# A state-space layer and a spectral layer on one core: stores moved to another queue, deeper loads, constants loaded ahead, and one image kept on the chip between the last stages

## The chip, the core and the metric

The kernel runs on one core of one Trainium2 chip. The time is device microseconds of the whole execution; the median of the runs counts. The profiled execution is a run of its own, with its own time.

The core's engines are TensorE (PE, matmuls; PEld is its weight load), VectorE (DVE), ScalarE (ACT), GpSimd (POOL) and SyncE (SP), which here only issues DMAs. Each engine works through its own queue in order. A DMA is issued by an instruction in one engine's queue and carried out by 16 DMA engines that all queues share.

## The reference, cut to what matters

Two layers on x of 4 images x 128 channels x 128 x 128 in float32. The first is a windowed state-space (Mamba) layer, which the change leaves alone. The second is this:

```python
z = (x - mu) / jnp.sqrt(var + 1e-05)          # over the channels
z = z * ln_gamma + ln_beta
Xf = jnp.fft.rfft2(z, axes=(-2, -1))          # 128 x 65 frequencies
Uf = Xf[:, :, None] * jnp.conj(Phi)[None, None]   # 16 filters Phi
U = jnp.fft.irfft2(Uf, s=(gx, gy), axes=(-2, -1))
S = jnp.einsum('bdlxy,lhd->bhxy', U, Theta)   # 16 matrices Theta, 128 x 128
H = jnp.einsum('bdxy,hd->bhxy', S, W1) + b1
H = jax.nn.gelu(H)
out = x + jnp.einsum('bhxy,dh->bdxy', H, W2) + b2
```

As everything up to S is linear, the kernel mixes the channels in the frequency domain: for each of the 65 frequency rows it multiplies the spectrum by the 16 Thetas and sums the products weighted by Phi, and transforms back only the sum.

## The kernel before, in words

Four functions run one after the other and hand over through DRAM.

`mamba_layer` (L34) writes the first layer's output `x1` and the normalised `z`, one DRAM tensor for each image (`zb[b]`). All of its loads and stores go through SP's queue.

`spectra` (L470) transforms one image after the other. For each image it goes through the 128 channels in groups of DG = 16; `load` (L493) brings one group's z tile (128 x 16 x 128, 1 MB, in rows of 512 bytes) two groups ahead, into three buffers. `along_x` (L499) takes four channels at a time: matmuls into a PSUM tile `p1`, then one copy into `a` (L504). `copies` alternates between ScalarE and VectorE. When all channels are in `a`, `along_y` (L506) transforms along y, three columns at a time, into a PSUM tile `p2`, and ScalarE copies its real half and VectorE its imaginary half into `x` (L517). `p1` and `p2` have four buffers each. `x` holds half an image's columns (q = 0 or 1); after each half it is stored to `xf` in one DMA of 4160 KB on SP's queue (L533), in rows of 512 bytes.

`mix` (L536) loads Theta and Phi (L549 to L552), then loops over the 65 rows. A row's `xk` is loaded two rows ahead in two DMAs (L561). For each of 16 filters PE multiplies (L584), and the results are weighted and summed by VectorE into `acc` (L599, L601), or, for six of the filters, weighted by ScalarE into `part` (L595) and summed by GpSimd into `apart` (L597). `finish` (L563) adds the two sums (L566) and stores the row for each image and half to `sf` in eight DMAs of 64 KB (L570). It runs after filter 5 of the next row, and once more after the last row.

`images_and_mlp` (L608) loads its constants (L624 to L630) and, for each image, the two halves of the mixed spectrum, 4160 KB each (L636), two buffers deep. `reorder` (L638) puts 16 channels at a time in order, ScalarE and VectorE sharing the work (L645 to L647); `along_x` (L649) and `along_y` (L661) transform back, and `hidden` and `project` are the MLP. The residual `x1` is loaded into `mx` (L665), the result is summed into `mo` (L688) and stored (L690).

Each function opens its own pools of on-chip memory and closes them at its end; the next function's pools take over the same memory. Waits are put in by the framework, from what each instruction reads and writes. `manual_schedule` keeps the order of the work near that in which the code lists it.

Of the kernel before, what the change touches and what calls it, by code (L numbers as in the profile page):

```python
# [13 lines left out]
F32 = mybir.dt.float32  # L14
# [7 lines left out]
WS = 8  # L22
# [5 lines left out]
HB = 512  # L28
NL = 16
KY = W // 2 + 1  # L30
NG = WS * W // P


def mamba_layer(tc, d, x, x1, zb, deltas, dus):  # L34
# [432 lines left out]
            go(lates.get(s, ()))  # L467


def spectra(tc, d, zb, xf):  # L470

    nc = tc.nc
    B = len(zb)
    DG = 16
    CG, KG = HB // W, HB // (2 * KY)
    WH = W // 2  # L480
    with ExitStack() as ctx:
        ctx.enter_context(tc.manual_schedule())
        cp = ctx.enter_context(tc.tile_pool(name="f_const", bufs=1))
        sb = ctx.enter_context(tc.tile_pool(name="f_sb", bufs=2))
        ps = ctx.enter_context(tc.tile_pool(name="f_ps", bufs=4, space=PSUM))
        fx = cp.tile([P, W], F32, tag="fx", name="fx")
        nc.sync.dma_start(fx, d["dft_x"])
        fy = cp.tile([P, 4 * KY], F32, tag="fy", name="fy")
        nc.sync.dma_start(fy, d["dft_y"])
        loaded = {}  # L490
        copies = itertools.cycle((nc.scalar.copy, nc.vector.tensor_copy))

        def load(b, i):  # L493
            b, i = b + i // P, i % P
            if b < B:
                loaded[b, i] = sb.tile([P, DG, W], F32, tag="z", name="z", bufs=3)
                nc.sync.dma_start(loaded[b, i], zb[b][i : i + DG].rearrange("c x y -> x c y"))

        def along_x(b, i, a):  # L499
            z = loaded[b, i - i % DG]  # L500
            p1 = ps.tile([P, CG, W], F32, tag="p1", name="p_fx")
            for k in range(CG):
                nc.tensor.matmul(p1[:, k], z[:, i % DG + k], fx, start=True, stop=True)
            next(copies)(a[:, :, i : i + CG].rearrange("p k c -> p c k"), p1)  # L504

        def along_y(a, x, cols):  # L506
            p2 = ps.tile([P, KG, 2 * KY], F32, tag="p2", name="p_fy")
            for o, k in zip(range(KG), cols):
                m = min(k, W - k)
                single = m % WH == 0  # L510
                nc.tensor.matmul(p2[:, o], a[:, m], fy[:, KY : 3 * KY], start=True, stop=single)
                if not single:
                    by = fy[:, : 2 * KY] if m == k else fy[:, 2 * KY :]
                    nc.tensor.matmul(p2[:, o], a[:, WH + m], by, start=False, stop=True)
            n, at = len(cols), cols[0] % WH
            for r in range(2):
                next(copies)(  # L517
                    x[:, :, r, at : at + n].rearrange("p y k -> p k y"), p2[:, :n, r * KY : (r + 1) * KY]
                )

        load(0, 0)
        load(0, DG)
        for b in range(B):
            a = sb.tile([P, W, P], F32, tag="a", name="a", bufs=1)
            for i in range(0, P, CG):
                if i % DG == 0:
                    load(b, i + 2 * DG)
                along_x(b, i, a)
            for q in range(2):
                x = sb.tile([P, KY, 2, WH], F32, tag="x", name="x")  # L530
                for k in range(q * WH, (q + 1) * WH, KG):
                    along_y(a, x, range(k, min(k + KG, (q + 1) * WH)))
                nc.sync.dma_start(xf[:, :, b, q].rearrange("y c r x -> c y r x"), x)  # L533


def mix(tc, d, xf, sf):  # L536

# [4 lines left out]
    APART = (1, 4, 6, 9, 12, 14)  # L542
    with ExitStack() as ctx:
        ctx.enter_context(tc.manual_schedule())
        cp = ctx.enter_context(tc.tile_pool(name="m_const", bufs=1))
        sb = ctx.enter_context(tc.tile_pool(name="m_sb", bufs=3))
        ps = ctx.enter_context(tc.tile_pool(name="m_ps", bufs=4, space=PSUM))
        theta = cp.tile([P, NL, P], F32, tag="theta", name="theta")
        nc.sync.dma_start(theta, d["Theta"])  # L549
        phi = cp.tile([P, 3, NL, KY], F32, tag="phi", name="phi")  # L550
        nc.sync.dma_start(phi[:, 0], d["Phi_r"])
        nc.sync.dma_start(phi[:, 1], d["Phi_i"])  # L552
        nc.vector.tensor_scalar(phi[:, 2], phi[:, 1], -1.0, None, ALU.mult)
        rows = {}

        def load(y):
            if y < KY:
                rows[y] = o = SimpleNamespace()
                o.xk = sb.tile([P, B, 2, 2, W // 2], F32, tag="xk", name="xk")
                for q in range(2):  # L560
                    nc.sync.dma_start(o.xk[:, :, :, q], xf[y, :, :, q])  # L561

        def finish(y):  # L563
            if y >= 0:
                o = rows.pop(y)
                nc.vector.tensor_tensor(o.acc, o.acc, o.apart, ALU.add)  # L566
                at = y - 1 if 0 < y < KY - 1 else KY - 2 + y // (KY - 1)
                for b in range(B):
                    for q in range(2):
                        nc.sync.dma_start(sf[b][:, q, at], o.acc[:, b, :, q * (P // 2) : (q + 1) * (P // 2)])  # L570

        load(0)
        load(1)
        for y in range(KY):
            o = rows[y]
# [29 lines left out]
        finish(KY - 1)  # L605


def images_and_mlp(tc, d, sf, x1, out):  # L608

# [7 lines left out]
    n = WS * W  # L617
    with ExitStack() as ctx:
        ctx.enter_context(tc.manual_schedule())
        cp = ctx.enter_context(tc.tile_pool(name="i_const", bufs=1))  # L620
        sb = ctx.enter_context(tc.tile_pool(name="i_sb", bufs=2))
        ps = ctx.enter_context(tc.tile_pool(name="i_ps", bufs=2, space=PSUM))
        ix = cp.tile([P, 2 * W], F32, tag="ix", name="ix")
        nc.sync.dma_start(ix, d["idft_x"])  # L624
        iy = cp.tile([P, W], F32, tag="iy", name="iy")
        nc.sync.dma_start(iy, d["idft_y"])
        c = {}
        for k in ("W1", "b1", "W2", "b2"):
            c[k] = cp.tile(list(d[k].shape), F32, tag=k, name=f"c_{k}")
            nc.sync.dma_start(c[k], d[k])  # L630
        spec, ordered, px, rows = {}, {}, {}, {}

        def load(b, q):
            if b < B:
                spec[b, q] = sb.tile([P, KY, 2, HP], F32, tag="s", name="s")
                nc.sync.dma_start(spec[b, q], sf[b][:, q])  # L636

        def reorder(b, i):  # L638
# [43 lines left out]
        def project(b, k, g):  # L682
            o = rows[b, k // 2]
            hs = slice(k % 2 * HB, (k % 2 + 1) * HB)
            po = ps.tile([P, HB], F32, tag="po", name="p_o")
            for m in range(2):
                nc.tensor.matmul(po, c["W2"][:, m], g[:, m], start=(m == 0), stop=(m == 1))  # L687
            nc.vector.scalar_tensor_tensor(o.o[:, hs], po, c["b2"], o.x[:, hs], ALU.add, ALU.add)  # L688
            if k % 2:
                nc.sync.dma_start(out[b][:, o.at].rearrange("c x y -> c (x y)"), o.o)  # L690
# [114 lines left out]
```

## Time and profile before

| | |
|---|---|
| median of 3 runs | 10520.61 us (10503.9 to 10534.1) |
| profiled execution, its own time | 10535.09 us |
| its span, first to last instruction | 10533.3 us |
| `mamba_layer`, about | 0 to 7273 us |
| `spectra`, PE's part | 7281 to 7683 us, PE busy 352.0 of 401 us |
| seam to `mix` | 7683 to 7709 us, PE busy 0.06 of 26 us |
| `mix`, PE's part | 7709 to 9711 us, PE busy 1941 of 2002 us |
| seam to `images_and_mlp` | 9711 to 9738 us, PE busy 0.8 of 27 us |
| `images_and_mlp` | 9738 to 10533 us, PE busy 786 of 796 us |

The profile is one execution. Its timeline lists instructions in order of time: start, duration, engine, line, what is written from what, how often, and in square brackets how long the engine had been idle and what released it. SPq and ACTq are the DMA issues in the queues of SP and ACT; the duration there is that of issuing, not of moving the data. The chain that ended last is followed back from the last instruction, at each step to what released it. A stretch lists for each engine its busy time and count, then the clock granted to TensorE as a share of full speed, the busy share of the DMA engines, and GB/s.

### The profile page before, as it was taken

To read this page: it belongs to the slowest core of one execution; us is meant where nothing else is said; L and a number is where in the kernel's file an instruction comes from. 1 tells how busy PE (TensorE), PEld (TensorE's weight loads), DVE (VectorE), ACT (ScalarE), POOL (GpSimd) and SP (SyncE) were. 2 spreads that over 40 slices of the span, in tenths; PEclk is the share of its full clock that TensorE was granted. 3 is DMA by queue.
4 is the path that set the end of the run, shared out by engine and by line. 5 is a ranking of instruction groups with operands and counts; after the bars stand their busy time and mean duration, and the time that the engine had idled before them with its cause. 6 is when DMAs were issued, how large, how long until landed. Compare 5 with 4: busy or idle time off the path is not lost.

```text
span 10533.3 us, 134916 instructions
## 1 busy us (share of the span) xinstructions
PE 9299.8 (88%) x46084; PEld 4658.4 (44%) x46084; DVE 9052.1 (86%) x7299; ACT 6333.5 (60%) x9711; POOL 8393.2 (80%) x4380
## 2 busy tenths in 40 slices
PE   7888888888888888888888888888889999998999
PEld 2222222222222222222222222224889999998766
DVE  6999999999999999999999999996379999998433
ACT  5766766766666666667667666664344444444433
POOL 5999899899999998999998999994069999998000
PEclk9999999999999999999999999998999999999999
DMA  5777777777777777777777777775621111112332
GB/s 156 210 216 210 207 215 211 207 218 206 214 216 205 216 211 204 221 212 208 215 211 207 216 207 216 214 205 159 169 69 35 35 35 35 35 35 63 133 128 93
DMA packets 1149630, 1759.95 MB, mean 167 GB/s; under 512 B 366592, under 2 KB 434448, under 8 KB 1147792
## 3 DMA queue, kind: packets, MB, share of 16 engines
q1 hardware_dynamic: 1148944, 1751.32, 58.7%
q8 instruction: 367, 6.01, 0.2%
q14 instruction: 319, 2.61, 0.1%
HBM read 1447.89 MB, written 303.04 MB: 166 GB/s over the span
## 4 chain that ended last, share of the span: by engine, by line
PE 46%; DVE 29%; ACT 12%; issue 6%; POOL 5%; DMA 2%; DVEq 0%; SPq 0%; ACTq 0%; POOLq 0%
DVE hs L416 19%; PE p_v L584 13%; PE p_conv L203 9%; DVE p_du L414 8%; ACT part L595 5%; PE p_du L382 4%; POOL hs L424 3%; PE p_out L275 2%; PE p_h L678 2%; PE p_o L687 2%; ACT dA L397 2%; PE p_y L434 2%; ACT p_du L397 2%; PE p_out L273 2%; PE p_in L189 1%
## 5 line engine op out<-in xcount | busy, mean ns | idle before, releaser
L424 POOL TENSOR_TENSOR hs<-hs,bc 128x1024 f32<-128x1024 f32 x2048 | 4797.4, 2361 | 469.8 <-DVE hs L416 464.9
L416 DVE TENSOR_TENSOR_SCAN hs<-dA,p_du 128x1024 f32<-128x1024 f32 x1664 | 3805.0, 2287 | 219.2 <-DVE p_du L414 3.4
L597 POOL TENSOR_TENSOR acc<-acc,part 128x512 f32<-128x512 f32 x1430 | 1829.3, 1319 | 615.3 <-ACT part L595 615.3
L414 DVE TENSOR_TENSOR p_du<-p_du,bc 128x1024 f32<-128x1024 f32 x1664 | 2014.8, 1211 | 273.9 <-PE p_du L382 270.1
L397 ACT ACTIVATE dA<-dr,A 128x504 f32<-128x504 f32 x3328 | 2156.0, 703 | 104.5 <-DVE hs L416 86.8
L584 PE MATMUL p_v<-theta,xk 128*128 128x128 f32 x16640 | 1941.4, 277 | 87.3 <-ACT part L595 51.4
L584 PEld LDWEIGHTS p_v<-theta,xk 128*128 128x128 f32 x16640 | 1883.1, 192 | 145.6 <-ACT part L595 118.3
L382 PE MATMUL p_du<-du,c_rsel 32*128 32x512 f32 x6656 | 1515.6, 662 | 478.6 <-DVE hs L416 473.4
L601 DVE SCALAR_TENSOR_TENSOR acc<-p_v,phi,acc 128x512 f32<-128x512 f32 x2470 | 1672.8, 741 | 114.3 <-PE p_v L584 87.4
L595 ACT ACTIVATE part<-p_v,phi 128x512 f32<-128x512 f32 x1430 | 903.7, 685 | 804.4 <-PE p_v L584 802.1
L434 PE MATMUL p_y<-hs,c_ssel 128*32 128x512 f32 x8192 | 1176.0, 642 | 189.3 <-DVE yz L264 185.7
L203 PE MATMUL p_conv<-tn,W_conv 128*128 128x512 f32 x2048 | 1007.5, 616 | 132.6 <-ACT zs L194 127.2
L382 PEld LDWEIGHTS p_du<-du,c_rsel 32*128 32x128 f32 x6656 | 409.1, 187 | 1532.1 <-issue 1004.7
L362 POOL TENSOR_TENSOR ur<-ur,bc 128x1024 f32<-128x1024 f32 x384 | 908.0, 2365 | 7.2 <-DMA ur<-du 7.2
L416 DVE TENSOR_TENSOR_SCAN hs<-p_du,ur 128x1024 f32<-128x1024 f32 x384 | 870.9, 2268 | 42.1 <-ACT p_du L397 29.4
L208 ACT ACTIVATE xc<-p_conv,b_conv 128x512 f32<-128x512 f32 x256 | 176.3, 689 | 829.2 <-PE p_conv L203 829.2
L434 PEld LDWEIGHTS p_y<-hs,c_ssel 128*32 128x32 f32 x8192 | 176.7, 110 | 1032.7 <-issue 728.6
L203 PEld LDWEIGHTS p_conv<-tn,W_conv 128*128 128x128 f32 x2048 | 347.0, 189 | 584.7 <-ACT zs L194 281.8
L228 PE MATMUL p_dt<-xc,W_dt 128*128 128x512 f32 x1024 | 535.0, 647 | 75.8 <-ACT dl L239 71.1
L218 PE MATMUL p_bc<-xc,c_W_bc 128*128 128x512 f32 x1024 | 501.3, 612 | 113.9 <-ACT dl L239 66.3
L397 ACT ACTIVATE p_du<-dr,A 128x504 f32<-128x504 f32 x768 | 526.1, 685 | 25.0
L246 POOL TENSOR_TENSOR dl<-dl,ab 128x1024 f32<-128x1024 f32 x128 | 303.3, 2370 | 178.1 <-ACT ab L243 178.1
(102 smaller groups left out, 9762.3 us busy)
## 6 DMA issues: line engine op xcount, KB each, us to landing
dr<-delta SPq DMA_DIRECT2D x4096, 256.0 KB, 4.8
ur<-du SPq DMA_DIRECT2D x768, 256.0 KB, 5.9
delta<-dl SPq DMA_DIRECT2D x128, 512.0 KB, 3.0
du<-du SPq DMA_DIRECT2D x128, 512.0 KB, 4.4
xf<-x SPq DMA_DIRECT2D x8, 4160.0 KB, 16.4
xk<-xf SPq DMA_DIRECT2D x130, 256.0 KB, 3.7
sf<-acc SPq DMA_DIRECT2D x520, 64.0 KB, 1.7
s<-sf SPq DMA_DIRECT2D x8, 4160.0 KB, 13.5
```

The costliest lines, as they stand in the source:

```text
L203: nc.tensor.matmul(windows(o.pc), W_conv[:, ch, k], moved, start=(k == 0), stop=(k == K - 1))
L362: nc.gpsimd.tensor_tensor(fetched[s], fetched[s], both(o.bc[0], h), ALU.mult)
L382: nc.tensor.matmul(u.bank[:, j % 2], c["rsel"][p, u.i], half(u.o.du[p, u.ch], u.h), start=True, stop=True)
L397: nc.scalar.activation(u.dA[:, q, :, 1:], u.delta[:, q].rearrange("p (w t) -> p w t", t=L)[:, :, 1:], AF.Exp, scale=A[:, g : g + 1],)
L414: nc.vector.tensor_tensor(u.bu, u.bu, both(u.o.bc[0], u.h), ALU.mult)
L416: nc.vector.tensor_tensor_scan(u.hs.rearrange("p q t -> p (q t)"), u.dA.rearrange("p q w t -> p (q w t)"), u.bu.rearrange("p q t -> p (q t)"),
L424: nc.gpsimd.tensor_tensor(u.hs, u.hs, both(u.o.bc[1], u.h), ALU.mult)
L434: nc.tensor.matmul(o.py[h, ch][32 * j : 32 * j + 32], c["ssel"][:, u.i], units[s + j // 2].hs[:, j % 2], start=(u.i == 0), stop=False, ski ...
L584: nc.tensor.matmul(t[:, b], o.xk[:, b, r], theta[:, k], start=True, stop=True)
L595: nc.scalar.activation(part, v[of], AF.Copy, scale=factor)
L597: nc.gpsimd.tensor_tensor(apart, apart, part, ALU.add)
L601: nc.vector.scalar_tensor_tensor(mine, v[of], factor, mine, ALU.mult, ALU.add)
```

## The change

In `spectra`, z is loaded four groups ahead instead of two, into five buffers instead of three. `xf` becomes five DRAM tensors of 13 rows each, and the half image's store becomes five DMAs issued by ScalarE. `mix` and `images_and_mlp` get their constants from tiles that are loaded during the first image's `spectra`, except Phi, which `mix` now loads after its first row. The first image's mixed rows go into two on-chip tiles `kept`, which `images_and_mlp` uses as its first two spectrum buffers; so `finish` adds in three pieces and stores three images instead of four. `images_and_mlp` sums into `mx`, which has three buffers instead of two, and `mo` is gone.

```diff
@@ spectra
-    DG = 16
+    DG, AHEAD = 16, 4
...
-                loaded[b, i] = sb.tile([P, DG, W], F32, tag="z", name="z", bufs=3)
+                loaded[b, i] = sb.tile([P, DG, W], F32, tag="z", name="z", bufs=AHEAD + 1)
...
-        load(0, 0)
-        load(0, DG)
+        for i in range(AHEAD):
+            load(0, i * DG)
...
-                    load(b, i + 2 * DG)
+                    load(b, i + AHEAD * DG)
                 along_x(b, i, a)
+            if b == 0:
+                preload()
             for q in range(2):
                 x = sb.tile([P, KY, 2, WH], F32, tag="x", name="x")
                 for k in range(q * WH, (q + 1) * WH, KG):
                     along_y(a, x, range(k, min(k + KG, (q + 1) * WH)))
-                nc.sync.dma_start(xf[:, :, b, q].rearrange("y c r x -> c y r x"), x)
+                for g, rows in enumerate(xf):
+                    nc.scalar.dma_start(rows[:, :, b, q].rearrange("y c r x -> c y r x"), x[:, g * YG : (g + 1) * YG])
@@ mix
-        theta = cp.tile([P, NL, P], F32, tag="theta", name="theta")
-        nc.sync.dma_start(theta, d["Theta"])
-        phi = cp.tile([P, 3, NL, KY], F32, tag="phi", name="phi")
...
+        theta = c["Theta"]
...
-                    nc.sync.dma_start(o.xk[:, :, :, q], xf[y, :, :, q])
+                    nc.sync.dma_start(o.xk[:, :, :, q], xf[y // YG][y % YG, :, :, q])
...
-                nc.vector.tensor_tensor(o.acc, o.acc, o.apart, ALU.add)
                 at = y - 1 if 0 < y < KY - 1 else KY - 2 + y // (KY - 1)
-                for b in range(B):
+                for q in range(2):
+                    hs = slice(q * (P // 2), (q + 1) * (P // 2))
+                    nc.vector.tensor_tensor(kept[q][:, at], o.acc[:, 0, :, hs], o.apart[:, 0, :, hs], ALU.add)
+                nc.vector.tensor_tensor(o.acc[:, 1:], o.acc[:, 1:], o.apart[:, 1:], ALU.add)
+                for b in range(1, B):
                     for q in range(2):
                         nc.sync.dma_start(sf[b][:, q, at], o.acc[:, b, :, q * (P // 2) : (q + 1) * (P // 2)])
         load(0)
+        phi = sb.tile([P, 3, NL, KY], F32, tag="phi", name="phi", bufs=1)
+        nc.sync.dma_start(phi[:, 0], d["Phi_r"])
+        nc.sync.dma_start(phi[:, 1], d["Phi_i"])
+        nc.vector.tensor_scalar(phi[:, 2], phi[:, 1], -1.0, None, ALU.mult)
         load(1)
@@ images_and_mlp
-        spec, ordered, px, rows = {}, {}, {}, {}
+        spec, ordered, px, rows = {(0, q): t for q, t in enumerate(kept)}, {}, {}, {}
...
-                spec[b, q] = sb.tile([P, KY, 2, HP], F32, tag="s", name="s")
+                spec[b, q] = sp.tile([P, KY, 2, HP], F32, tag="s", name="s")
...
-                o.x = sb.tile([P, n], F32, tag="mx", name="mx")
+                o.x = sb.tile([P, n], F32, tag="mx", name="mx", bufs=3)
...
-                o.o = sb.tile([P, n], F32, tag="mo", name="mo")
...
-            nc.vector.scalar_tensor_tensor(o.o[:, hs], po, c["b2"], o.x[:, hs], ALU.add, ALU.add)
+            nc.vector.scalar_tensor_tensor(o.x[:, hs], po, c["b2"], o.x[:, hs], ALU.add, ALU.add)
...
-        load(0, 0)
-        load(0, 1)
@@ conv_kernel
-    xf = tc.dram_tile([KY, P, B, 2, 2, W // 2], F32, name="xf")
+    xf = [tc.dram_tile([min(YG, KY - y), P, B, 2, 2, W // 2], F32, name=f"xf_{y}") for y in range(0, KY, YG)]
...
-    spectra(tc, d, zb, xf)
-    mix(tc, d, xf, sf)
-    images_and_mlp(tc, d, sf, x1, out)
+    cp = ctx.enter_context(tc.tile_pool(name="tail_const", bufs=1))
+    c = {k: cp.tile(list(d[k].shape), F32, tag=k, name=f"c_{k}") for k in "Theta idft_x idft_y W1 b1 W2 b2".split()}
+
+    def preload():
+        for k, t in c.items():
+            tc.nc.sync.dma_start(t, d[k])
+
+    spectra(tc, d, zb, xf, preload)
+    sp = ctx.enter_context(tc.tile_pool(name="tail_spec", bufs=2))
+    kept = [sp.tile([P, KY, 2, P // 2], F32, tag="s", name="s") for _ in range(2)]
+    mix(tc, d, c, xf, sf, kept)
+    images_and_mlp(tc, c, sp, kept, sf, x1, out)
```

More of the change, by code (lines that the diff above doesn't have):

```diff
@@ L30 @@
 KY = W // 2 + 1
-NG = WS * W // P
+YG = 13
 def mamba_layer(tc, d, x, x1, zb, deltas, dus):
@@ L467, in mamba_layer, with spectra @@
             go(lates.get(s, ()))
-def spectra(tc, d, zb, xf):
+def spectra(tc, d, zb, xf, preload):
     nc = tc.nc
     B = len(zb)
-    DG = 16
+    DG, AHEAD = 16, 4
     CG, KG = HB // W, HB // (2 * KY)
@@ L532, in spectra, with mix @@
                     along_y(a, x, range(k, min(k + KG, (q + 1) * WH)))
-                nc.sync.dma_start(xf[:, :, b, q].rearrange("y c r x -> c y r x"), x)
-def mix(tc, d, xf, sf):
+                for g, rows in enumerate(xf):
+                    nc.scalar.dma_start(rows[:, :, b, q].rearrange("y c r x -> c y r x"), x[:, g * YG : (g + 1) * YG])
+def mix(tc, d, c, xf, sf, kept):
     nc = tc.nc
@@ L544, in mix @@
         ctx.enter_context(tc.manual_schedule())
-        cp = ctx.enter_context(tc.tile_pool(name="m_const", bufs=1))
         sb = ctx.enter_context(tc.tile_pool(name="m_sb", bufs=3))
         ps = ctx.enter_context(tc.tile_pool(name="m_ps", bufs=4, space=PSUM))
-        theta = cp.tile([P, NL, P], F32, tag="theta", name="theta")
-        nc.sync.dma_start(theta, d["Theta"])
-        phi = cp.tile([P, 3, NL, KY], F32, tag="phi", name="phi")
-        nc.sync.dma_start(phi[:, 0], d["Phi_r"])
-        nc.sync.dma_start(phi[:, 1], d["Phi_i"])
-        nc.vector.tensor_scalar(phi[:, 2], phi[:, 1], -1.0, None, ALU.mult)
+        theta = c["Theta"]
         rows = {}
@@ L605, in mix, with images_and_mlp @@
         finish(KY - 1)
-def images_and_mlp(tc, d, sf, x1, out):
+def images_and_mlp(tc, c, sp, kept, sf, x1, out):
     nc = tc.nc
@@ L619, in images_and_mlp @@
         ctx.enter_context(tc.manual_schedule())
-        cp = ctx.enter_context(tc.tile_pool(name="i_const", bufs=1))
         sb = ctx.enter_context(tc.tile_pool(name="i_sb", bufs=2))
         ps = ctx.enter_context(tc.tile_pool(name="i_ps", bufs=2, space=PSUM))
[L623 to L630, printed above, removed]
-        spec, ordered, px, rows = {}, {}, {}, {}
+        ix, iy = c["idft_x"], c["idft_y"]
+        spec, ordered, px, rows = {(0, q): t for q, t in enumerate(kept)}, {}, {}, {}
         def load(b, q):
             if b < B:
-                spec[b, q] = sb.tile([P, KY, 2, HP], F32, tag="s", name="s")
+                spec[b, q] = sp.tile([P, KY, 2, HP], F32, tag="s", name="s")
                 nc.sync.dma_start(spec[b, q], sf[b][:, q])
@@ L687, in project @@
                 nc.tensor.matmul(po, c["W2"][:, m], g[:, m], start=(m == 0), stop=(m == 1))
-            nc.vector.scalar_tensor_tensor(o.o[:, hs], po, c["b2"], o.x[:, hs], ALU.add, ALU.add)
+            nc.vector.scalar_tensor_tensor(o.x[:, hs], po, c["b2"], o.x[:, hs], ALU.add, ALU.add)
             if k % 2:
-                nc.sync.dma_start(out[b][:, o.at].rearrange("c x y -> c (x y)"), o.o)
-        load(0, 0)
-        load(0, 1)
+                nc.sync.dma_start(out[b][:, o.at].rearrange("c x y -> c (x y)"), o.x)
         reorder(0, 0)
```

## The prediction

> **What bounds the kernel now.** I read the busy time by slices first: TensorE (PE) is 70 to 99% busy in every one, and no slice shows a gap. So I took the chain that ended last, in order of time, over the last three stages:
>
> ```profile
> 7372.74 19.87 DMA z<-z
> ...
> 7475.52 20.07 DMA z<-z
> ...
> 7579.83 19.88 DMA z<-z
> ...
> 7682.53 16.11 DMA xf<-x
> 7700.76 7.98 DMA xk<-xf
> ...
> 9721.99 12.63 DMA s<-sf
> ```
>
> Everything else on it is PE work. The change aims at these six pieces: three loads between images in `spectra`, the seam to `mix`, the seam to `images_and_mlp`. PE's timeline says what they cost PE (each matmul leaves two records; 32 records are one 16-channel z tile):
>
> ```profile
> 7371.23 7.31 PE L503 MATMUL p_fx<-fx,z 128*128 128x128 f32 x64
> 7392.74 12.43 PE L503 MATMUL p_fx<-fx,z 128*128 128x128 f32 x95 [14.21 <-DMA z<-z]
> ```
>
> PE still had two tiles and then idled 14.2 us, not 20. Why the third tile was late stands in SP's queue, from the same moment and from the start of the stage:
>
> ```profile
> 7372.15 0.38 SPq L533 DMA_DIRECT2D xf<-x  x1
> 7372.74 12.68 SPq L497 DMA_DIRECT2D z<-z  x1
> ```
> ```profile
> 7274.84 0.76 SPq L497 DMA_DIRECT2D z<-z  x1
> 7276.06 1.25 SPq L497 DMA_DIRECT2D z<-z  x1
> 7277.78 3.08 SPq L497 DMA_DIRECT2D z<-z  x1
> ```
>
> A store is issued in 0.38 us, but the transfer behind it holds its queue for 12.68 us, although its buffer had long been free. The third of three loads holds it for 3.08. The stretches show the rate and the clock (last columns: granted clock, DMA share, GB/s):
>
> ```profile
> 7376.00:7380.00 4.00, 2.54 (x23) 2.34 (x21) 2.10 (x3) 1.96 (x2) 0.00 (x0) 1.00 1.04 290
> 7392.00:7395.00 3.00, 2.26 (x10) 2.29 (x11) 0.00 (x0) 0.18 (x1) 0.00 (x0) 0.50 1.05 289
> ```
>
> So 512-byte rows move at 290 GB/s and no faster, and after the idle time PE runs at half clock until about 7396.4: some 3.6 us, 1.8 lost. One image seam costs 14.2 + 1.8 = 16.0 us.
>
> From rate and holds a rule follows. The store is 4.26 MB; data started near 7373.1, and the next command was accepted at 7385.42, when 12.3 x 0.29 = 3.57 MB had gone: about 0.7 MB was still queued. For the third load: by 7280.86 some 1.3 of the two earlier loads' 2.1 MB had gone, 0.8 queued. **A queue takes a command only when all but about 0.75 MB of the rows ahead of it has moved.**
>
> **What the Trainium skill says.** "Perfetto Trace Analysis", section "DMA Instruction — HWDGE (DVE, Sync)": the descriptor generator is shared and locked, and the issuing sequencer isn't free until it is done. The trace agrees in kind (12.68 us), but it is the next command that pays. "DMA: Bandwidth & Descriptors", section "Issuing engines are not separate DMA queues": issue time is "usually small relative to the DMA itself"; here it was 12.68 beside a store of 16.4. "TensorE: Matmul & The Clock Gate", section "What's actually happening": an idle window of about 3.4 us drops the clock; here it fell about 3.9 us after PE's last matmul.
>
> **Part 1, five stores from ScalarE's queue.** Each half image now issues five pieces of 0.852 MB on ACT's queue, behind ACT's last copy of that half and in front of its first of the next. No row shows a DMA issued by ACT. Lower bound: five issues at 0.38, 1.9 us. Upper: SP's rule, and I take it. The fifth piece is accepted once four pieces less 0.75 MB have gone: (3.41 - 0.75)/0.29 = 9.2, with 1.0 until data flows and an issue 0.4: ACT is held **10.5 us**. Queued behind it are ACT's copies out of PSUM, and VectorE's wait for those:
>
> ```profile
> 7342.62 0.72 ACT L517 COPY x<-p_fy 128x195 f32<-128x195 f32 x2 [0.84 <-PE p_fy L514]
> ```
> ```profile
> 7343.15 0.61 DVE L517 COPY x<-p_fy 128x195 f32<-128x195 f32 x2 [0.84 <-ACT x L517]
> ```
>
> PE is covered only by its four PSUM buffers.
> - First half (4 times): the store goes out 0.5 us after PE begins the second half. Four tiles last 4 x 1.34 = 5.4 us; the fifth waits until 0.5 + 10.5 + 1.1 for the two copies = 12.1. Stall 6.7, and the idle time is long enough for the half clock: + 1.8 = 8.5; four of them **+34**.
> - Second half (3 times; the last has no next image): four p_fx tiles last 3.6 us; the fifth waits until 0.9 + 10.5 + 1.25 = 12.7: stall 9.1. One z load of 1.05 MB is released after these four tiles and shares the DMA engines: up to + 3.6, which I take: 12.7 + 1.8 = 14.5; three of them **+43.5**.
>
> **Part 2, loads four deep, own queue.** Five z tiles of the next image are in before its seam, and SP no longer stands behind a store. The three seams go: 3 x 16.0 = **-48**. The first image's 1.1 us stall goes too: **-1**. Late next is what part 1 says. The constants (1.5 MB on SP, 5 us at 290 GB/s) fall into the first image's second transform, 57 us of PE work with little else to load: nothing; without that cover, 5 us.
>
> **Part 3, spectra to mix.** Splitting `xf` lets row 0 depend on the first piece only. But does it also wait for memory? The waits of SP's queue:
>
> ```profile
> SPq L549 <- DMA xf<-x: 15.6, 1, 15.6
> ```
> ```profile
> SPq L624 <- DVE acc L601: 13.1, 1, 13.1
> ```
>
> Theta reads an input, yet it waited for the store out of x; `ix`, small enough to lie over theta alone, waited for VectorE's last use of phi. So a new pool's tiles wait until every tile of the pools they overlap is released. The new `xk` lies in a pool over `spectra`'s, so it still waits for the last piece to land, 16.4 us. What goes is what stood ahead of it: theta, phi. Before, 10.0 us from the first issue to PE's start; after, two issues of 1.0 and a landing of 3.7: 5.7. Phi now comes behind xk; VectorE starts 2 to 3 us earlier, within PE's eight PSUM buffers: **-4** (with tile-wise release it would be -13).
>
> **Part 4, mix to images.** PE waits 26.7 us for its first matmul at 9737.17. The end of `mix`:
>
> ```profile
> 9715.09 1.23 DVE L566 TENSOR_TENSOR acc<-acc,acc 128x1024 f32<-128x1024 f32 x1 [2.52 <-POOL acc L597]
> ```
> ```profile
> 9716.34 3.96 SPq L570 DMA_DIRECT2D sf<-acc  x8
> ```
>
> After: the add in three pieces (0.2 + 0.2 + 0.95, scaled from 1.23) ends at 9716.5. Six stores at 0.5 end at 9719.5, and land 1.7 after the last issue, 9720.8. The reordered tile lies over mix's pool, so it waits for that; then VectorE's two copies, 1.16 + 1.07, and 0.2: PE at 9723.2. **-14** (-18 with tile-wise release). In the other rows of `mix` the split add costs VectorE some 0.1 us beside a PE that is 97% busy, and two store issues of 0.5 fewer on SP: nothing, as SP is mostly idle there.
>
> **Part 5, images.** `mx` three deep and the sum written into it: the buffer comes free when its store has landed (2.9 us), and three rows (some 27 us) pass before it is used again. PE is 98.8 to 100% busy there: nothing.
>
> **Sum**: 34 + 43.5 - 48 - 1 - 4 - 14 = **+10** against 10535.1 (span 10533.3 and 1.8 around it). That execution lies 14.5 above the median of the runs, 10520.6, all parts of it alike, so I add to the median: **10530**, where 0.3% is 32 us, about what a measurement of this kernel can tell from no change.
>
> **Rivals.**
> - *ScalarE's queue isn't held* (1.9 us in place of 10.5). For it: a lone store takes 0.38 us, and ACT is another queue. Against: the three holds above. First-half stalls vanish; second-half ones are 0.9 + 1.9 + 1.25 - 3.6, about 0.5, and a late z load perhaps 1 more: 5 in all. -48 - 1 + 5 - 18 = -62: 10459. Faster.
> - *The hold is longer*: ACT is held until the fifth piece is through, 16.4 us like the whole store. For it: the skill's description, where the command's own descriptors count. Against: 0.38 us for the store itself. Stalls 12.6 + 1.8 (4) and 18.6 + 1.8 (3): 119 - 49 - 18 = +52: 10572. It turns slower by over 0.3% from a hold of about 13.7 us, as seven stalls grow with it.
> - *Row-wise xk works* (tile-wise release, no z contention): 9 + 4 + 11 less: 10506. No change still.
>
> **Numbers.** My case (hold 8 to 13 us, with either release) 0.57, its own range 10500 to 10552; queue not held, or hardly (under 5 us), 0.26; longer hold 0.17. The range takes in the unheld queue: 10457 to 10554. Faster 0.28 (with holds near 5), same 0.54, slower 0.18.
>
> **What would show it.** DMA issues on ACT in fives, the last three some 3 us each; PE stalls of 6 to 7 us in mid-image, released by ACT's x copies, and about 12 us at the image seams, released by ACT's copy of `a` and not by z; xk issued 16 us after the last half; PE idle 13 us before p_ix. Wrong: fives of 0.4 us each with no stall (first rival), or a fifth that takes as long as the store (second).

## The result, and the profile after

The kernel after takes 10538.40 us in the median (10526.12 to 10547.02, 20 runs), the kernel before, run in turn with it on the same chip, 10528.92. The ratio is 1.001, with a 95% interval of 1.0003 to 1.0017: some 10 us slower, within the 0.3% that the prediction called no change. The forecast was 10530.

A sum of large terms with both signs can come out right by luck, so the terms are looked at one by one. Both profiled executions differ by chance in `mamba_layer`, which the change leaves alone (PE's first matmul of `spectra` begins at 7281.3 us before, at 7273.1 after), so stages are compared from there on. The profile's `p_fx` and `p_fy` are the tiles in PSUM, the memory that matmuls write, of `along_x` and `along_y` in `spectra`; `p_v` is that of `mix`, `p_ix` the first of `images_and_mlp`. A seam is the stretch between two stages or two images. Worked out from the starts of the first and the last matmul of each stage, in us (one execution each):

| | spectra | seam to mix | mix | seam to images | images | from first p_fx to end |
|---|---|---|---|---|---|---|
| before | 400.2 | 27.4 | 2001.3 | 27.0 | 796.1 | 3252.0 |
| after | 427.0 | 22.6 | 2005.2 | 12.8 | 796.6 | 3264.2 |
| difference | +26.8 | -4.8 | +3.9 | -14.2 | +0.5 | +12.2 |
| predicted | +28.5 | -4 | 0 | -14 | 0 | +10 |

Here are pieces of the chain that ended last after the change, in order of time; they answer to the six DMA pieces shown of before:

```profile
7266.47 6.44 DMA z<-z
7273.15 30.78 PE p_fx L503 x256
...
7374.78 12.32 DMA xf<-x
...
7709.01 8.50 DMA xf<-x
7718.46 4.00 DMA xk<-xf
```

The loads of `z` between the images are gone (the one shown is the first of the stage). In their place stands a store, `xf<-x`, which no later instruction of `spectra` reads: it can be on the chain only because something queues behind it. The timeline of the kernel after, at the middle of the first image, says what:

```profile
7333.82 0.61 DVE L517 COPY x<-p_fy 128x195 f32<-128x195 f32 x2 [0.84 <-ACT x L517]
7334.47 10.68 ACTq L536 DMA_DIRECT2D xf<-x  x5
7345.19 1.47 ACT L517 COPY x<-p_fy 128x195 f32<-128x195 f32 x4 [11.17 <-DMA xf<-x]
7345.71 1.48 DVE L517 COPY x<-p_fy 128x195 f32<-128x195 f32 x4 [11.27 <-ACT x L517]
7346.24 0.80 PE L511 MATMUL p_fy<-fy,a 128*128 128x130 f32 x2 [7.40 <-DVE x L517]
```

Read it downwards. ScalarE's queue issues the five stores (ACTq) and is held 10.68 us. Its next copy out of PSUM starts only then, VectorE's half of the same tile behind it, and PE, which had filled its four PSUM buffers, idles 7.40 us. The chain of the kernel after breaks the hold into its commands:

```profile
7334.90 1.05 ACTq L536
7335.99 3.15 ACTq L536
7339.18 2.98 ACTq L536
7342.20 2.95 ACTq L536
```

The first two take 1.5 us together (7334.47 to 7335.99), each later one 3 us, which is the time in which 0.85 MB, one piece, moves at the 290 GB/s seen before (0.85 / 0.29 = 2.9). So a command is taken when the bytes ahead of it have shrunk far enough, as the prediction's rule has it. The four holds in mid-image are 10.50 to 10.70 us, the three at the image seams 13.57 to 13.77.

At the seam from the first image to the second (the timeline after):

```profile
7372.50 4.63 PE L503 MATMUL p_fx<-fx,z 128*128 128x128 f32 x40
7373.43 13.62 ACTq L536 DMA_DIRECT2D xf<-x  x5
7377.36 1.16 PE L503 MATMUL p_fx<-fx,z 128*128 128x128 f32 x8 [0.23 <-DVE a L504]
7379.62 1.16 PE L503 MATMUL p_fx<-fx,z 128*128 128x128 f32 x8 [1.10 <-DVE a L504]
7387.09 3.62 ACT L504 COPY a<-p_fx 128x512 f32<-128x512 f32 x4 [14.10 <-DMA xf<-x]
7388.15 4.21 PE L503 MATMUL p_fx<-fx,z 128*128 128x128 f32 x18 [7.37 <-ACT a L504]
```

The z tiles are there, and PE still idles 8.7 us in three parts, the longest 7.37: the releaser is now ScalarE's copy, not a DMA. The clock pays as well; these stretches of the kernel after follow the stall at mid-image (the granted clock is the last column but two):

```profile
7347.00:7349.00 2.00, 2.00 (x11) 2.00 (x10) 0.18 (x1) 0.00 (x0) 0.00 (x0) 0.50 1.05 288
7351.00:7353.00 2.00, 2.00 (x14) 2.00 (x14) 0.49 (x1) 0.49 (x1) 0.00 (x0) 0.67 0.00 0
7353.00:7355.00 2.00, 2.00 (x21) 2.00 (x20) 0.50 (x1) 0.67 (x2) 0.00 (x0) 1.00 0.00 0
```

The two seams, in SP's queue and PE's timeline after: `xk` and then the first matmul of `mix`, and the end of `mix` up to the first matmul of `images_and_mlp`:

```profile
7717.79 1.37 SPq L559 DMA_DIRECT2D xk<-xf  x2
```
```profile
7722.71 12.49 PE L589 MATMUL p_v<-c_Theta,xk 128*128 128x128 f32 x88 [22.31 <-DMA xk<-xf]
```
```profile
9732.61 0.49 DVE L567 TENSOR_TENSOR s<-acc,acc 128x128 f32<-128x128 f32 x2 [1.35 <-POOL acc L602]
9733.02 0.95 DVE L568 TENSOR_TENSOR acc<-acc,acc 128x768 f32<-128x768 f32 x1
9738.41 1.17 DVE L643 COPY so<-s 128x1040 f32<-128x1040 f32 x1 [4.44 <-DMA sf<-acc]
9740.69 0.77 PE L653 MATMUL p_ix<-c_idft_x,so 128*128 128x128 f32 x2 [12.53 <-DVE so L644]
```

The kept spectrum was complete at 9733.1, yet the copy that reads it started 5.3 us later, when the last stores of `sf`, which it has no use for, had landed. That it waited for memory, as the prediction had it for the reordered tile, is what an experiment below tests.

One group differs where nothing was expected, in `mix` (groups from 7735 to 9700 us; the last columns are busy time, mean ns of one, and idle time ahead). Before:

```profile
L601 DVE SCALAR_TENSOR_TENSOR acc<-p_v,phi,acc 128x512 f32<-128x512 f32 x2425 | 1642.5, 741 | 111.2 <-PE p_v L584 84.8
L566 DVE TENSOR_TENSOR acc<-acc,acc 128x1024 f32<-128x1024 f32 x64 | 143.5, 2242 | 0.0
```

After:

```profile
L606 DVE SCALAR_TENSOR_TENSOR acc<-p_v,phi,acc 128x512 f32<-128x512 f32 x2423 | 1611.6, 738 | 4.2 <-PE p_v L589 2.7
L567 DVE TENSOR_TENSOR s<-acc,acc 128x128 f32<-128x128 f32 x126 | 160.6, 1313 | 0.0
L568 DVE TENSOR_TENSOR acc<-acc,acc 128x768 f32<-128x768 f32 x63 | 126.1, 2002 | 0.0
```

An add of an eighth of the width takes 1313 ns, not an eighth of 2242. The adds of one row now cost VectorE 2 x 1.31 + 2.00 = 4.6 us, not 2.24, and its idle time in this stage fell from 111.2 to 4.2 us. The longer `mix` isn't chance: four kernels below that leave this part of `mix` as after take 2004.2 to 2005.1 us there, and one that leaves `mix` as before takes 2001.2.

### The profile page after: what moved, and what is told of

Its sections match the earlier page's. It is cut to its first block, busy times and chain, and to the rows that moved or that the text cites. A ratio compares the mean times of both kernels' runs of the same rounds, so it can differ in the third digit from the quotient of the medians.

```text
span 10537.3 us, 134843 instructions
## 1 busy us (share of the span) xinstructions
PE 9316.3 (88%) x46084; PEld 4671.8 (44%) x46084; DVE 9162.7 (87%) x7429; ACT 6333.5 (60%) x9711; POOL 8381.8 (80%) x4380
## 4 chain that ended last, share of the span: by engine, by line
PE 42%; DVE 29%; ACT 12%; issue 8%; POOL 7%; DMA 1%; ACTq 1%; DVEq 0%; SPq 0%; POOLq 0%
DVE hs L416 19%; PE p_conv L203 9%; PE p_v L589 9%; DVE p_du L414 8%; ACT part L600 5%; PE p_du L382 4%; POOL hs L424 3%; PE p_out L275 2%; ACT dA L397 2%; POOL acc L602 2%; PE p_h L674 2%; PE p_o L683 2%; PE p_y L434 2%; ACT p_du L397 2%; PE p_out L273 1%
## 5 line engine op out<-in xcount | busy, mean ns | idle before, releaser
L602 POOL TENSOR_TENSOR acc<-acc,part 128x512 f32<-128x512 f32 x1430 | 1818.9, 1312 | 651.6 <-ACT part L600 651.6
L589 PE MATMUL p_v<-c_Theta,xk 128*128 128x128 f32 x16640 | 1942.4, 277 | 85.4 <-ACT part L600 51.9
L589 PEld LDWEIGHTS p_v<-c_Theta,xk 128*128 128x128 f32 x16640 | 1883.6, 192 | 144.2 <-ACT part L600 118.9
L606 DVE SCALAR_TENSOR_TENSOR acc<-p_v,phi,acc 128x512 f32<-128x512 f32 x2470 | 1643.0, 738 | 5.3 <-PE p_v L589 3.7
```

Source lines behind the costliest of these rows:

```text
L589: nc.tensor.matmul(t[:, b], o.xk[:, b, r], theta[:, k], start=True, stop=True)
L602: nc.gpsimd.tensor_tensor(apart, apart, part, ALU.add)
L606: nc.vector.scalar_tensor_tensor(mine, v[of], factor, mine, ALU.mult, ALU.add)
```

## The experiments

The theory: a DMA queue takes its next command only when about 0.75 MB of what is ahead of it is left; ScalarE stands behind the pieces of its own store, and that hold, not the loads, now sets `spectra`; at the two seams between stages the first tiles wait for whole pools of memory. All edits are against the kernel after unless another is named. Stage times that are quoted come from the same working as the table above. Each ratio is to the kernel before, run in turn on the same chip.

**The same five pieces from SP's queue.** This takes the hold off ScalarE and leaves everything else.

```diff
-                    nc.scalar.dma_start(rows[:, :, b, q].rearrange("y c r x -> c y r x"), x[:, g * YG : (g + 1) * YG])
+                    nc.sync.dma_start(rows[:, :, b, q].rearrange("y c r x -> c y r x"), x[:, g * YG : (g + 1) * YG])
```

> The changed kernel with its five pieces per half image issued from SP's queue again, nothing else undone. Theory (ScalarE is held by its own queue, and its PSUM copies behind it): no DMA issue and no idle time of 7 us in mid-image, so the four first-half losses of 10.6 us go (-42). At the image seams ScalarE copies at once, but the sixth z tile now stands behind the pieces in SP's queue: it lands some 22 us after the seam where PE has work for 18, so 4 to 6 us are left of 12: -18 to -24 for three. Together -60 to -66 against the changed kernel, about 10475. Rival (the loss comes from moving 4.26 MB beside the work, whichever queue issues it): the mid-image idle time stays, within 10 us of the changed kernel.

10489.19 us, ratio 0.9958 (0.9945 to 0.997): the direction is the forecast one, the gain smaller than the 60 to 66 us expected. `spectra` took 378.7 us, 48.3 less than after, and no stall is left at mid-image. The hold is still there, on SP, where no copy stands behind it:

```profile
7384.10 11.45 SPq L536 DMA_DIRECT2D xf<-x  x5
```
```profile
7383.18 14.46 PE L503 MATMUL p_fx<-fx,z 128*128 128x128 f32 x128
7405.00 16.23 PE L503 MATMUL p_fx<-fx,z 128*128 128x128 f32 x128 [7.37 <-DMA z<-z]
```

PE runs 128 records, four z tiles, and waits 7.37 us for the fifth; the forecast had it wait for the sixth. A fifth tile isn't in ahead of the seam here: its load is listed in the next image's first step, so in SP's order it comes behind the stores. The prediction's "five z tiles are in before the seam" holds after only because the stores are on another queue. So five pieces in ScalarE's queue cost 48 us more than five in SP's, and leaving SP has a use of its own.

**One store for a half image, from ScalarE's queue.** If the next command pays, a store with nothing behind it on its queue but copies is free.

```diff
-YG = 13
+YG = 65
```

> The changed kernel with xf as one tensor and one store of 4160 KB per half, from ScalarE's queue. Theory (it is the next command of a queue that pays for the rows ahead of it): one store is issued in 0.4 us and nothing follows it on ScalarE for 29 us, so ScalarE isn't held: no stall in mid-image (-42) and hardly any at the seams (-30 to -36), 10455 to 10470. Rival (a queue is held by the bytes of its own command, so by 4.26 MB for 10 us or more): stalls as in the changed kernel, within 10 us of it. If the two queues share one generator of descriptors, SP's z loads at the seams are accepted only some 12 us after the store, and the gain at the seams shrinks to about half.

10478.20 us, ratio 0.9946 (0.9934 to 0.9959). The same bytes from the same queue, and ScalarE goes on at once (timeline of this kernel):

```profile
7359.35 0.39 ACTq L536 DMA_DIRECT2D xf<-x  x1
7359.77 0.49 ACT L517 COPY x<-p_fy 128x195 f32<-128x195 f32 x1 [0.88 <-PE p_fy L514]
```

`spectra` takes 355.0 us, 72.0 less than after and 45.2 less than before. SP's next z load goes out 2.9 us after the second store (7390.60, the store 7387.71) in 0.68 us: the store didn't hold the other queue for the 12 us that the expectation allowed for. Nor does the store hold the engine that issues it; it holds a further command behind it on the same queue.

**Two pieces, and thirteen.** These give the size of the hold.

```diff
-YG = 13
+YG = 33
...
-                    nc.scalar.dma_start(rows[:, :, b, q].rearrange("y c r x -> c y r x"), x[:, g * YG : (g + 1) * YG])
+                    nc.scalar.dma_start(rows[:, :, b, q].rearrange("y c r x -> c y r x"), x[:, g * YG : min((g + 1) * YG, KY)])
```

> The changed kernel with two pieces (33 and 32 rows, 2.16 and 2.10 MB) from ScalarE's queue. Theory with the rule of 0.75 MB: the second piece is accepted when all but 0.75 MB of the first has moved, (2.16 - 0.75)/0.29 + 1.4 = 6.3 us of hold, in place of 10.7; PE's four tiles cover 5.4 us, so about 2.5 us of idle time are left in mid-image, too little for the half clock: -8 each, -32 for four; at the seams some -4 each, -12: about -44, 10495. Rival (a hold that depends on the number of commands, about 2 us each): 4 us of hold, no idle time in mid-image, some 10480.

10493.00 us, ratio 0.9961 (0.9948 to 0.9973). ScalarE's queue and PE in mid-image, for two pieces:

```profile
7343.66 6.17 ACTq L536 DMA_DIRECT2D xf<-x  x2
```
```profile
7350.93 0.49 PE L511 MATMUL p_fy<-fy,a 128*128 128x130 f32 x2 [2.89 <-DVE x L517]
```

Hold and stall are as forecast. Not so the clock: two of the four mid-image stalls, of 2.89 and 2.78 us, did bring 3.41 us of half clock; the other two, of 2.93 and 2.83 us, brought none.

For thirteen pieces of 0.33 MB:

```diff
-YG = 13
+YG = 5
```

> The changed kernel with 13 pieces of 5 rows (0.33 MB each) per half in place of 5, from ScalarE's queue. Theory (the hold is set by the bytes ahead of the last command: all but 0.75 MB of the first twelve pieces' 3.93 MB): 3.18/0.29 + 1.4 = 12.4 us of hold in mid-image in place of 10.7, PE idle 9 us there in place of 7.4, so about 4 x 1.7 + 3 x 1.7 = 12 us slower than the changed kernel, some 10550. Rival (the hold grows with the number of commands, 2 to 3 us for each beyond the second): 25 us or more of hold, 10630 or more.

10557.25 us, ratio 1.0021 (1.0012 to 1.003), and ScalarE's queue shows:

```profile
7347.11 13.18 ACTq L536 DMA_DIRECT2D xf<-x  x13
```

Four kernels, one store, 1, 2, 5 and 13 commands: ScalarE is held 0.39, 6.17, 10.68 and 13.18 us at the first mid-image, and within 0.2 us of that at the other three. The rule of 0.75 MB gives 0.4, 6.3, 10.6 and 12.4 from the bytes ahead of the last piece. A cost for each further command, (10.68 - 0.39) / 4 = 2.6 us, would have given 3.0 at two and 31 at thirteen, and falls. Thirteen pieces show 0.8 more than the rule; a small part for each command isn't excluded. All rows here have 512 bytes, so whether bytes or rows are counted isn't shown.

**The kept image's add in one instruction.** The two adds of 128 columns become one of 256, and the kept tile one tile with both halves.

```diff
-                for q in range(2):
-                    hs = slice(q * (P // 2), (q + 1) * (P // 2))
-                    nc.vector.tensor_tensor(kept[q][:, at], o.acc[:, 0, :, hs], o.apart[:, 0, :, hs], ALU.add)
+                first, apart = (v[:, 0].rearrange("p r (q x) -> p q r x", q=2) for v in (o.acc, o.apart))
+                nc.vector.tensor_tensor(kept[:, :, at], first, apart, ALU.add)
```

> The changed kernel with the first image's two adds of 128x128 made one of 128x256 (the two kept buffers are one tile), so finish has two adds on VectorE, not three. Theory (each VectorE add of two SBUF operands beside GpSimd's adds costs 1.3 us whatever its size, so the split costs VectorE 2.4 us a row and takes its slack): VectorE's adds take about 3.4 us a row in place of 4.6, its idle time in mix is back to some 50 us or more, and mix is 2 to 4 us shorter, 10534 to 10537. Rival (mix is longer because phi comes late at its start, not because of the adds): mix stays at 2005 us.

10540.22 us, ratio 1.0007 (0.9998 to 1.0015): as a time, this can't be told from the kernel after. The stage tells more. `mix` takes 2001.7 us, against 2005.2 after and 2001.3 before, and VectorE has idle time again (groups in `mix`, the same stretch):

```profile
L605 DVE SCALAR_TENSOR_TENSOR acc<-p_v,phi,acc 128x512 f32<-128x512 f32 x2424 | 1635.5, 741 | 47.8 <-PE p_v L588 27.1
L566 DVE TENSOR_TENSOR s<-acc,acc 128x256 f32<-128x256 f32 x63 | 89.7, 1424 | 0.0
```

Twice the columns cost 1424 ns, not 2 x 1313. So 3.5 of the 3.9 us in `mix` go with one add a row, and it is the number of adds that costs, not their width.

**`xk` and the reordered tile in pools of their own.** The theory has both seams wait for memory, not for data. Here both tiles lie in pools that overlap nothing of the stage before: `xk` in one opened ahead of `spectra`, the reordered tile in one opened ahead of `mix`.

```diff
+    xp = ctx.enter_context(tc.tile_pool(name="tail_xk", bufs=3))
     spectra(tc, d, zb, xf, preload)
+    op = ctx.enter_context(tc.tile_pool(name="tail_so", bufs=2))
...
-                o.xk = sb.tile([P, B, 2, 2, W // 2], F32, tag="xk", name="xk")
+                o.xk = xp.tile([P, B, 2, 2, W // 2], F32, tag="xk", name="xk")
...
-                t = ordered[b, i] = sb.tile([P, CB, 3 * KY - 2], F32, tag="so", name="so")
+                t = ordered[b, i] = op.tile([P, CB, 3 * KY - 2], F32, tag="so", name="so")
```

> The changed kernel with two buffers in pools of their own: xk in a pool opened ahead of spectra, and the reordered tile (so) in one opened ahead of mix, so that neither lies over memory of the stage before. Theory (a new pool's tiles wait until all of the pools they lie over are released): row 0's xk is issued some 6 us after the last half image's stores begin, not 16.4, and PE begins mix 12 to 15 us after its last p_fy, not 22.6 (phi still lies over spectra's pool and lands late, so VectorE begins at 24 as before, and PE runs ahead of it by its eight buffers, so that up to 5 us of the gain are lost again); the reorder no longer waits for the six stores to sf, so p_ix begins 8 to 9 us after p_v's end, not 12.8. Together some -8 to -12. Rival (the data's own way through DRAM is what is late): both seams stay at 22.6 and 12.8.

10531.68 us, ratio 1.0002 (0.9994 to 1.0011). The seams take 12.6 and 8.3 us in place of 22.6 and 12.8; the same data is read as soon as it is there. At the second one (timeline of this kernel), VectorE's add releases the first reordering copy at once, with no store between:

```profile
9751.46 4.12 ACT L642 ACTIVATE so<-s 128x1040 f32<-128x1040 f32 x2 [4.64 <-DVE s L567]
9754.70 0.77 PE L653 MATMUL p_ix<-c_idft_x,so 128*128 128x128 f32 x2 [8.03 <-issue]
```

But `mix` took 2010.3 us, 5.1 more, so that a third of the 14.5 gained at the seams was given back. PE started 10 us earlier and soon stood still; phi was the last thing that VectorE waited for (21.8 us, by the waits). Phi still lay in a pool over `spectra`'s memory: its load went out at 7741.29, just after the last piece of the store had landed (7741.14), although the last load of row 0 had gone out at 7728.95, when the first piece had. That phi's lateness is the whole of the 5 us is argued from that. In the next kernel, where phi is loaded ahead along with other edits, the seam and `mix` together less PE's one wait are 2018.8 - 16.2 = 2002.6 us, which agrees.

**All that helped, together.** One store for a half image from ScalarE; only the last half, which has no copies behind it, in five pieces, from SP; one add for the kept image; both tiles in pools of their own; phi among the constants loaded ahead. To make room, `mx` shares `xk`'s buffers, and a row's `xk` is now loaded in three DMAs. The central edit:

```diff
+                if (b, q) == (B - 1, 1):
+                    for g, rows in enumerate(last):
+                        nc.sync.dma_start(rows.rearrange("y c r x -> c y r x"), x[:, g * YG : (g + 1) * YG])
+                else:
+                    nc.scalar.dma_start(xf[q][:, :, b].rearrange("y c r x -> c y r x"), x)
...
+    xf = [tc.dram_tile([KY, P, B - q, 2, W // 2], F32, name=f"xf_{q}") for q in range(2)]
+    last = [tc.dram_tile([YG, P, 2, W // 2], F32, name=f"xl_{y}") for y in range(0, KY, YG)]
```

> What the runs so far point to, in one kernel: one store for each half image from ScalarE's queue; the last half alone in five pieces, from SP's queue, where nothing stands behind them; xk and so in pools of their own; phi loaded with the other constants; one add for the kept rows; mx in xk's memory. Theory: spectra 355 us, seam to mix 12 to 14 us, mix 2001 to 2003, seam to images 8 to 9, images 796: the part from the first p_fx on is some 3174 to 3178 us, 75 us less than before (3252.0), so about 10455. Rival (gains don't add, since a shorter seam lets VectorE and GpSimd fall behind at mix's start and mix grows by what the seam lost): 3186 or more.

10453.73 us, ratio 0.9925 (0.9911 to 0.9939): the shortest of all. From the first p_fx to the end it takes 3178.9 us, 73.1 less than before and 85.3 less than after. `spectra` is down to 354.8. PE's waits at the seam missed the forecast, though:

```profile
PE p_v L588 <- DMA xk<-xl: 16.2, 1, 16.2
```

16.2 us, not 12 to 14: the load of row 0's last part stands in SP's queue behind the five pieces (it goes out at 7649.21, after their 10.57 us), so it pays the hold that ScalarE no longer pays. The expectation had overlooked that the loads of `mix` share this queue.

**The last pieces from ScalarE instead.** The remedy for that, against the kernel just shown.

```diff
-                        nc.sync.dma_start(rows.rearrange("y c r x -> c y r x"), x[:, g * YG : (g + 1) * YG])
+                        nc.scalar.dma_start(rows.rearrange("y c r x -> c y r x"), x[:, g * YG : (g + 1) * YG])
```

> The kernel of e6 with one change: the last half image's five pieces go out from ScalarE's queue, not SP's. In e6 the load of mix's first row stood behind those pieces in SP's own queue and PE waited 16.2 us. Theory: the load is now issued when the first piece has landed, some 6 us after PE's last p_fy, and PE waits 9 to 11 us; ScalarE is held 10.5 us, but mix first needs it some 13 us after, so that costs nothing: 5 to 7 us less than e6 from the first p_fx on, 3172 to 3174 us, about 10448. Rival (ScalarE's hold delays mix's first copies, or mix gives back what the seam gains as VectorE is its bound): within 2 us of e6.

10472.68 us, ratio 0.9943 (0.993 to 0.9955). The forecast of 5 to 7 us less failed: by that ratio it is no faster than the kernel just shown, and from the first p_fx to the end it takes 3182.0 us, 3.1 more in one execution each. PE's wait for the row fell to 9.0, and the time came back behind it (chain of this kernel):

```profile
7639.49 5.47 DMA xk<-xl
7644.98 8.88 DMA xl<-x
7654.09 1.26 ACT acc L599 x2
```

The row is there at 7645.0, and the first weighted product, `acc`, is written at 7654.1, when the last piece has landed. `acc` lies in the pool of `mix` over `spectra`'s memory, so this fits the pool theory; but a kernel with `acc` in a pool apart wasn't run, so for this wait it is argued and not shown.

**The deeper loads alone, on the kernel before.**

```diff
-    DG = 16
+    DG, AHEAD = 16, 4
...
-                loaded[b, i] = sb.tile([P, DG, W], F32, tag="z", name="z", bufs=3)
+                loaded[b, i] = sb.tile([P, DG, W], F32, tag="z", name="z", bufs=AHEAD + 1)
```

The loads ahead of the loop and in it reach four groups ahead to match, and the stores stay on SP.

> The kernel before with z loaded four groups ahead into five buffers, and nothing else. Theory (five tiles are in before a seam, one store of 16 us still stands ahead of the sixth in SP's queue, which lands some 22 us after the seam, where PE has work for 18): each seam loses 4 to 8 us instead of 16, so -25 to -35 in all and about 10500. Rival (z behind a store on the same queue costs the whole store whatever the depth, so the move to another queue was needed): within 5 us of before.

10504.50 us, ratio 0.9973 (0.9963 to 0.9983). `spectra` takes 377.2 us, 23 less than before; PE at the first image seam:

```profile
7362.17 14.46 PE L503 MATMUL p_fx<-fx,z 128*128 128x128 f32 x128
7384.36 17.02 PE L503 MATMUL p_fx<-fx,z 128*128 128x128 f32 x128 [7.73 <-DMA z<-z]
```

Half of the old stall is left, 7.7 of 14.2 us, with the fifth tile, not the sixth as forecast, behind the store. So the deeper loads gain about 23 us by themselves in `spectra` (27 between the medians), and the pieces on ScalarE's queue took that and more away.

## Why the prediction was right, and where its terms were off

The mechanism was the forecast one at each stall that the prediction named, and the rivals fell: ScalarE's queue is held (10.68 us, not 1.9), it isn't held for as long as the whole store (not 16.4), and row 0 does wait for the last piece (the xk load is issued at 7717.79, after the store's last 8.50 us on the chain). The sum was +10 and the measured one +12.2 in the profiled executions, +9.5 in the medians. The stated range took in the first rival as well, so the total alone would have shown nothing about the mechanism. By its steps:

- *First half of an image, +34.* The hold was put at 10.5 and was 10.68, PE's stall at 6.7 and was 7.40. The term that was mis-sized is the half clock, 1.8: PE ran at half clock from 7346.2 to 7352.3, 6.1 us, so about 3.0 were lost. The transform along y of one image, with the stall at its middle, takes 10.6 us longer than before the change (67.4 against 56.8), four of them 42.3. The Trainium skill's page "TensorE: Matmul & The Clock Gate", section "What's actually happening", on which the prediction drew, has the clock fall after an idle window of about 3.4 us and rise after a busy one, in windows that run freely and don't start with the work. The traces agree on the windows (the last section), but here a gap of 2.78 us, in the kernel with two pieces, already brought the clock down. The prediction took the time to rise from the one stall seen before, put at 3.6 us where the trace has 3.3, as if it were a constant.
- *Image seams, +43.5 and -48.* The half clock lasted longer than forecast here too, 5.1 us after the first seam's stall, but PE got further ahead than the four tiles counted: seven PSUM tiles (40 records and twice 8, at 8 a tile), because VectorE kept emptying its share of the tiles while ScalarE stood still. The idle time was 0.23 + 1.10 + 7.37 = 8.7, not the 12.7 that the prediction had. With 2.6 lost at half clock that is 11.3 us a seam, some 34 in all against 43.5. The hold, 13.62, was near the 14.1 that the prediction worked with; its "290 GB/s and no faster" holds for the store alone: with a z load from the other queue beside it the DMA engines moved 314 GB/s (7380 to 7387 us of the kernel after). The `along_x` of the three images behind a seam took 125.7 us in all after and 140.0 before, so the net of the seams was -14.3, not -4.5. That miss of 9.8 in favour cancelled the 8.3 of the first halves: `spectra` came out at +26.8 for +28.5, partly by luck.
- *First image and constants, -1 and nothing.* Right: the first image's `along_x` takes 31.96 us for 33.10 before, and `along_y` takes 67.40 us in the first image, with the constants' loads about it, and 67.37 in the second.
- *Seam to mix, -4, and to images, -14.* Right, -4.8 and -14.2. Of what the change left of the two waits, pools apart took away another 10.0 and 4.5 us, so memory was waited for there, as predicted. That theta loaded ahead and the kept image bring the -4.8 and -14.2 is read from the chains; no run undid either alone.
- *The split add, "some 0.1 us" in each row.* This step failed. It scaled the last row's 1.23 us, an add that began when GpSimd had just stopped. In the other rows an add costs 1.0 us more than alone, whatever its width: 1.31 for 0.28, 2.00 for 0.95, 2.24 for 1.23, so the split costs VectorE 2.4 us a row. The kernel before shows 2242 ns in the group's mean, beside 1.23 in the timeline; the prediction read only the latter. The Trainium skill's page "SBUF — State Buffer", section "SBUF: two separate sides", says that a VectorE instruction with two SBUF inputs and a GpSimd one that reads SBUF lock each other out for a whole instruction. The trace fits that: GpSimd's adds there take 1312 ns each and are in progress 91% of this stretch. PE is then not the sole bound in `mix`: VectorE's busy time rose from 1853.8 to 1960.8 of the 1965 us, and the 3.9 us go with it; with one add less, at 1915.4, they are nearly gone.

So the question where the gain went has an answer: the deeper loads alone bring `spectra` 23 us, and with one store from ScalarE's queue 45, against the kernel before; splitting the store put the hold in front of ScalarE's copies, in seven places, and cost 72.

## What to carry to other kernels

In these runs a large DMA command wasn't paid for by itself but by the next command on its queue, which waited for the bytes ahead to move. So on an engine that has compute work queued, a big store is better one command: in five pieces it cost ScalarE 10.7 us of a transfer of about 16.4. When a stage seam is slow, ask of each first instruction whether it waits for its data or for the memory under its own tile, and give all of the first tiles of a stage a pool that is already free; one left behind, as phi and perhaps `acc` here, can give the gain back. Price an operation that repeats from its group's mean, in the company it keeps, and not from one lone instance at the end.

## What the runs showed of the hardware that was not expected

- VectorE's adds of two on-chip operands beside a busy GpSimd: 1313, 1424, 2002 and 2242 ns for 128, 256, 768 and 1024 columns. Once GpSimd had stopped, 128 columns took 280 to 290 ns, 256 took 420, 768 took 950 and 1024 took 1230. The extra is about 1.0 us at each width; that it would go without GpSimd is seen only at the stage's last row, and no kernel without GpSimd's adds was run.
- The half clock after idle time: 6.1 us after a gap of 7.40, but 3.3 after a gap of 14.21. The traces show how the two differ. The stretches in which the clock falls and rises are these, in the first stall of the kernel before and then the first of the kernel after (whose rise, in the stretch from 7351 to 7353, is shown above):

```profile
7382.00:7383.00 1.00, 0.00 (x0) 0.00 (x0) 0.00 (x0) 0.00 (x0) 0.00 (x0) 0.71 1.04 291
7396.00:7397.00 1.00, 1.00 (x11) 1.00 (x10) 0.61 (x1) 0.00 (x0) 0.00 (x0) 0.96 1.04 287
```
```profile
7341.00:7343.00 2.00, 0.00 (x0) 0.00 (x0) 0.00 (x0) 0.00 (x0) 0.00 (x0) 0.77 1.07 289
```

The shares put the half clock at 7382.42 to 7396.08 before, 13.65 us, and 7342.08 to 7352.32 after, 10.24 us: four and three steps of 3.41. The other stalls of all the kernels from `spectra` on show whole steps too, on one beat through each execution. A restart within 0.4 us after a step was at full clock at the next one; a restart 0.65 us or more after it had to wait one step more. So recovery took 3.1 to 6.2 us, whatever the gap: PE's restart at 7392.74 came 0.08 us after a step, the one at 7346.24 came 0.75 after.

- The hold of ScalarE's queue for one store of 4.26 MB in 1, 2, 5 and 13 commands: 0.39, 6.17, 10.68 and 13.18 us.
